# Cosines multiplied on ScalarE, and layer 1's counts emitted later, in a two-layer kernel on one core

## The chip, the core and the metric

The kernel runs as one program on one core of one Trainium2 chip. The metric is the time of one execution on the device, in microseconds. Engines are named as in the profile: PE is TensorE (PEld its weight loads), DVE is VectorE, ACT is ScalarE, POOL is GpSimd, and SP is SyncE, which issues DMAs. A "q" behind a name (SPq, ACTq, POOLq) is that engine's issuing side.

## The reference, cut to what matters

There are two layers over 4 sequences of 1024 tokens with 256 features, all in fp32. In each, an attention part `s` and a mixture of experts `g` work on the same normalized tokens, and their gated product is added to the stream. In layer 0 the attention part is a gated recurrence over the sequence, and the experts are 16 of inner width 128. In layer 1 the projections are cosines, and the experts are 16 of inner width 64, with a shared expert of width 512 beside them. Both choose 4 experts per token, 2 in each of 2 chosen groups of 4 in layer 1.

```python
def _L1_attn_ref(x, theta, W_c, b_c):
    proj = jnp.cos(theta)[None, None] * jnp.cos(xh)        # xh: x by heads of 16
    proj = proj.reshape(Bb, Ss, E)
    scores = jnp.einsum('bse,bte->bst', proj, proj) / jnp.sqrt(jnp.asarray(D, x.dtype))
    attn = jax.nn.softmax(scores, axis=-1)
    out = jnp.einsum('bst,bte->bse', attn, proj)
    return out @ W_c.T + b_c
...
xn = _layernorm(x, axis=-1)
s = _L1_attn_ref(xn, L1_attn_theta, L1_attn_W_c, L1_attn_b_c)
g = _silu(_L1_ffn_ref(xn, L1_ffn_router_w, ...))
x = x + s * g
```

The change concerns the product `cos(theta) * cos(xh)` and the sorting of tokens by expert in `_L1_ffn_ref`.

## The kernel before, in words

**Tiles.** P is 128, S 1024, TB 512, D 256, so KC = 2 halves of the features. A sequence is a "batch" `b` of 0 to 3, worked in halves `q` of 512 tokens. `xnT` holds the normalized activations transposed, 2 x 128 x 1024, and `projT` the cosines in the same shape.

**Preparation.** `prep1(b)` (L967) makes projT and the values. For each half of the features and of the tokens `cos_reduced` (L173: rows L175, L177, L181 twice, L184) brings the angles into range on DVE. Then ACT takes the sine of both feature halves (L995; sine and sigmoid-like functions need different tables, so ACT_TABLE_LOAD rows stand around it). Then DVE multiplies each feature half, 128x1024, by a column of `cth` (L998). After that 32 matmuls on PE (L1006) make the values in PSUM, `projT` times `W_c`, and ACT copies them out (L1013). `val` goes to tiles shared with other users of the pool.

**Routing of layer 1.** `route1` (L908) normalizes (`norm_transposed`, L190: statistics L199 and L200, Newton steps L204 to L216 on DVE, then y on ACT at L226, transposes on PE at L235, copies L237 and L239), computes the logits, and leaves the choices of a batch in `em1` (L926). `places1(h)` (L933) is called for each of two groups of batches: `places` (L359) counts, with matmuls of `em` on PE (L370, L372) and then some forty small instructions on DVE (L376 to L443), at which row each token goes. `dispatch1(h)` (L936) then has POOL scatter the tokens' rows to `rows_in`, and the experts of layer 1 (L1179) work on them.

**Other work near it.** `experts` (L596) holds both layers' expert loop: it transposes a group of 128 rows (L630, copied by L634), multiplies by gate and up weights (L642), applies the gate (L468, L469, L653), transposes h (L659, copied by L661 on ACT), multiplies by the down weights (L667) and copies out (L679, L685); the store of rows is L718. `gathered` (L722) has POOL gather layer 0's expert rows (L725), and DVE adds them up (L790, L792), with a residual that is loaded by L112 as `g_half`. `attend(b)` (L1018) is the attention proper (L1059 to L1118, with L1033 to L1040 finishing a half), `share(b)` (L1127) the shared expert (products L1138 and L1154). `clears` (L841) writes zeros to `rows_in`. Layer 1's weights are loaded at L1360 to L1364.

**What sets the order.** Every such piece of work is a Python generator. It emits instructions and yields a number, the planned microseconds until its next piece. One main line of work at a time is run by `run` (L887), which moves a clock on by a fixed cost for every step (PAIR 0.81, ATTEND 1.4, SHARE 2.6, ROUTED 0.64), and lets the side lines, objects of class `Beside` (L867), emit what is due by then. SETTLED is 3.0 and PIECE is 1.0; both are only planner time and no instruction. A `Beside` has a `pace` with which its pauses are multiplied. The two side lines that concern the change are `routing`, which holds `places1` and `dispatch1`, with a pace of 0.7 from the end of layer 0's experts on, and `preparing`, which holds `prep1` for one batch. Batch 0 is prepared beside layer 0's experts, batches 1 and 2 beside the attention and the shared expert of the batch ahead of them, and batch 3 beside layer 1's experts:

```python
    for b in range(3):
        preparing = Beside(prep1(b + 1, "gu")) if b < 2 else Beside(loads1())
        run(attend(b), ATTEND, [*others, preparing])
        run(share(b), SHARE, [*others, preparing])
        if b < 2:
            together(preparing)
```

`behind` (L859) lets side work be issued after the newest instruction on each engine. Beyond this, a scheduler of the framework merges the emitted lists of each engine with its own idea of costs, so that a change of the emission moves instructions on several engines. An engine executes its own list in order, and pools of tiles (tags such as "x", "tp", "gu", "mm") set when a tile comes free.

Of the kernel before, what the change touches and what calls it, by code (L numbers as in the profile page):

```python
# [13 lines left out]
ALU = mybir.AluOpType  # L14
# [37 lines left out]
SETTLED = 3.0  # L52
PIECE = 1.0
# [10 lines left out]
def two_layer_kernel(  # L64
# [18 lines left out]
    nc = tc.nc  # L83
# [9 lines left out]
    def bank(tag, bufs):  # L93
        tag = side[0] if tag == "side" else tag
        return psum.tile([P, 512], F32, tag=tag, name=tag, bufs=bufs)
# [77 lines left out]
    def cos_reduced(dst, src, tmp, parts):  # L173

        nc.vector.tensor_scalar(tmp, src, INV_2PI, MAGIC, ALU.mult, ALU.add)  # L175
        yield
        nc.vector.tensor_scalar(tmp, tmp, MAGIC, None, ALU.subtract)  # L177
        yield
        at = src
        for part in parts:  # L180
            nc.vector.scalar_tensor_tensor(dst, tmp, -part, at, ALU.mult, ALU.add)  # L181
            at = dst
            yield
        nc.vector.scalar_tensor_tensor(dst, dst, -1.0, dst, ALU.mult, ALU.max)  # L184
# [57 lines left out]
    def transposed_tile():  # L242
        return work.tile([P, KC, S], F32, tag="xnT", name="xnT", bufs=3)
# [324 lines left out]
    def spent(us):  # L568

        clock[0] += us  # L570
# [358 lines left out]
    def tiles_of(h):  # L929

        return slice(GROUPS[h][0] * NT, (GROUPS[h][-1] + 1) * NT)

    def places1(h):  # L933
        placed1.append((yield from places(em1[:, tiles_of(h), :], G1 + h, WE1, "tp")))

    def dispatch1(h):  # L936
# [30 lines left out]
    def prep1(b, tag):  # L967

        if b < 2:
            while b not in turned:  # L970
                yield PIECE
            xnT = turned[b]
        else:
            while b not in routed_done:
                yield PIECE
            xnT = transposed_tile()
            nc.sync.dma_start(out=xnT.rearrange("p k s -> p (k s)"), in_=normedT[b])
            there = clock[0] + LANDING
            while clock[0] < there:
                yield PIECE  # L980
        if b == 1:

            projT = [work.tile([P, QUAD, D + INFO], F32, tag="q", name="projT", bufs=QB) for _ in range(KC)]
            projT = [t.rearrange("p i d -> p (i d)")[:, 0:S] for t in projT]
        else:
            projT = work.tile([P, KC, S], F32, tag="big_a", name="projT", bufs=1)
            projT = [projT[:, kc, :] for kc in range(KC)]
        for kc in range(KC):
            for cols in (slice(0, TB), slice(TB, S)):
                k = work.tile([P, TB], F32, tag="t", name="k", bufs=1)  # L990
                for _ in cos_reduced(projT[kc][:, cols], xnT[:, kc, cols], k, TWO_PI_NORMED):
                    pass
                yield 2 * PIECE
        for kc in range(KC):
            nc.scalar.activation(projT[kc], projT[kc], AF.Sin, bias=half_pi, scale=-1.0)  # L995
        yield PIECE
        for kc in range(KC):
            nc.vector.tensor_scalar(projT[kc], projT[kc], cth[:, kc : kc + 1], None, ALU.mult)  # L998
        yield 3 * SETTLED

        val = [xpool.tile([P, NS, D + INFO], F32, tag="x", name="val", bufs=XB)[:, :, 0:D] for _ in range(NQ)]
        for c in range(0, NT, 2):
            ps = bank(tag, 2)
            for i in range(2):
                for kc in range(KC):
                    nc.tensor.matmul(  # L1006
                        ps[:, i * D : (i + 1) * D],
                        lhsT=projT[kc][:, (c + i) * P : (c + i + 1) * P],
                        rhs=wc_sb[:, kc, :],
                        start=(kc == 0),  # L1010
                        stop=(kc == KC - 1),
                    )
            nc.scalar.copy(val[c // NS][:, c % NS : c % NS + 2, :], ps.rearrange("p (c d) -> p c d", d=D))  # L1013
            spent(1.7)
            yield PIECE
        ready[b] = xnT, projT, val
# [289 lines left out]
    cth = const.tile([P, KC], F32, tag="cth", name="cth")  # L1306
# [28 lines left out]
    def until(ready, *beside):  # L1335

        while not ready():
# [8 lines left out]
    routing = Beside(  # L1346
        then(
            *(step for h, bs in enumerate(GROUPS) for step in (routes1(bs, "side"), places1(h))),
            *(dispatch1(h) for h in range(len(GROUPS))),
        )  # L1350
    )
    preparing = Beside(prep1(0, "side"))
    with behind():
        run(experts0(), PAIR, [clearing, combined, routing, preparing])
# [21 lines left out]
# [6 lines that stand above are left out]
    until(lambda: len(placed1) == len(GROUPS) and preparing.done, *others, preparing)  # L1382
    preparing = Beside(prep1(3, "gu"))

    gating = Beside(then(*(gated1(b) for b in range(B))), 1.7)
# [72 lines left out]
```

## Time and profile before

| | |
|---|---|
| Times of three runs | 1134.44, 1134.29, 1133.79 us (median 1134.29) |
| The profiled execution's own time | 1132.03 us |
| Its span in the profile | 1130.3 us |
| Busy, DVE and POOL | 652.7 us (58%) and 564.4 us (50%) |
| Busy, weight loads of PE | 765.9 us (68%) |
| DMA | 264.82 MB, 234 GB/s over the span |
| Mean granted clock of PE | 0.957 |

The span is what the profiler's records cover, and the execution's own time has about 1.7 us around it. Busy times leave out waiting, issuing of DMAs and semaphores. A line of a timeline reads: start, length, engine, source line, operation, output and inputs, shape, count, and in brackets the idle time of the engine ahead of it with what ended it. "The chain" is the list of instructions and transfers that ended last, followed back from the end; its shares say which engine the time went through.

### The profile page before, as it was taken

The numbers are of one execution on the slowest core, as the hardware profiler recorded it, in microseconds if no ns is written. First come the engines' busy times: TensorE is split into PE (matmuls) and PEld (weight loads), VectorE is DVE, ScalarE is ACT, GpSimd is POOL, SyncE is SP. The second block draws the span as 40 slices with busy tenths as digits, with TensorE's granted clock in tenths as the row PEclk, the third lists the DMA queues.
The fourth block names the chain that finished last, engine by engine and source line by source line (L and its number), as shares of the span: only waits on it lengthen the run. The fifth ranks groups of instructions, "written<-read, shape, count | busy, mean of one in ns | idle before, by whom it ended". The sixth has DMA issues, their size and how long they took to land.

```text
span 1130.3 us, 16158 instructions
## 1 busy us (share of the span) xinstructions
PE 1029.2 (91%) x4928; PEld 765.9 (68%) x4928; DVE 652.7 (58%) x1967; ACT 463.9 (41%) x1028; POOL 564.4 (50%) x589
## 2 busy tenths in 40 slices
PE   5678699999899799979589999999999999999997
PEld 4245368888778688666357765776777777776675
DVE  4866963333688733067977884023733337776666
ACT  3345454444355444331223621221655555553132
POOL 1277377741770000377334677777756666776000
PEclk9868899999999899998699999999999999999999
DMA  8997569999999487997236553654555569994871
GB/s 338 401 410 265 172 191 324 308 310 250 313 346 263 136 215 189 342 246 196 84 119 217 181 175 130 215 196 158 179 170 186 190 215 351 359 332 145 274 242 38
DMA packets 118995, 264.82 MB, mean 234 GB/s; under 512 B 14208, under 2 KB 71680, under 8 KB 117632
## 3 DMA queue, kind: packets, MB, share of 16 engines
q1 hardware_dynamic: 78256, 138.79, 39.3%
q0 software_dynamic: 27264, 75.86, 19.9%
q10 hardware_dynamic: 13392, 49.14, 12.8%
q8 instruction: 43, 0.70, 0.3%
q14 instruction: 40, 0.33, 0.1%
HBM read 119.34 MB, written 144.39 MB: 233 GB/s over the span
## 4 chain that ended last, share of the span: by engine, by line
PE 64%; DVE 21%; DMA 7%; issue 3%; ACT 2%; POOL 2%; DVEq 0%; ACTq 0%; POOLq 0%
PE gu L642 14%; PE acc L667 10%; PE acc L1091 7%; PE tp L630 5%; PE gu L1138 4%; PE acc L1154 4%; PE mm L1138 4%; PE mm L1059 4%; DMA r<-rows_out,row 3%; PE tp L659 3%; PE acc L296 2%; DVE x_half L1243 2%; DMA rows_out<-o 2%; PE mm L514 1%; DVE stats L199 1%
## 5 line engine op out<-in xcount | busy, mean ns | idle before, releaser
L725 POOL DMA_INDIRECT r<-rows_out,row x128 | 130.6, 1021 | 237.5 <-issue 156.5
L642 PE MATMUL gu<-w_sb,xT 128*128 x1280 | 238.0, 329 | 1.5 <-ACT xT L634 0.9
L642 PEld LDWEIGHTS gu<-w_sb,xT 128*128 128x128 f32 x1280 | 193.9, 192 | 15.9 <-issue 2.2
L1205 POOL DMA_INDIRECT results<-o,dest x160 | 159.7, 998 | 76.9 <-issue 29.4
L582 POOL DMA_INDIRECT rows_in<-x_half,row x128 | 134.2, 1048 | 102.7 <-issue 52.4
L667 PE MATMUL acc<-w_sb,hT 128*128 (+1 forms) x640 | 180.1, 397 | 4.0 <-ACT hT L661 4.0
L469 DVE SCALAR_TENSOR_TENSOR h<-sg,gu 128x256 f32<-128x256 f32 (+1 forms) x160 | 56.0, 351 | 161.4 <-ACT sg L468 161.2
L582 POOL DMA_INDIRECT rows_in<-t_half,row x128 | 126.0, 985 | 40.6 <-issue 38.3
L667 PEld LDWEIGHTS acc<-w_sb,hT 128*128 128x128 f32 (+1 forms) x640 | 107.3, 189 | 31.9 <-issue 15.8
L1091 PE MATMUL acc<-val,es 128*128 128x256 f32 x512 | 127.9, 392 | 0.8 <-ACT es L1071 0.8
L634 ACT COPY xT<-tp 128x512 f32<-128x512 f32 x160 | 93.7, 586 | 73.8 <-PE tp L630 71.3
L1091 PEld LDWEIGHTS acc<-val,es 128*128 128x128 f32 x512 | 97.5, 198 | 24.3 <-issue 10.3
L630 PE MATMUL tp<-ident,xs 128*128 128x128 f32 x640 | 101.0, 281 | 0.0
L468 ACT ACTIVATE sg<-gu 128x256 f32<-128x256 f32 (+1 forms) x160 | 53.0, 331 | 113.7 <-PE gu L642 108.6
L630 PEld LDWEIGHTS tp<-ident,xs 128*128 128x128 f32 x640 | 74.4, 142 | 32.5 <-issue 18.1
L685 DVE COPY o<-acc 128x512 f32<-128x512 f32 x80 | 55.0, 688 | 61.4 <-PE acc L667 60.2
L659 PE MATMUL tp<-ident,h 128*128 128x128 f32 (+1 forms) x320 | 62.1, 276 | 10.1 <-DVE h L653 7.8
L1059 PE MATMUL mm<-projT 128*128 128x512 f32 (+3 forms) x192 | 70.0, 487 | 0.0
L661 ACT COPY hT<-tp 128x256 f32<-128x256 f32 (+1 forms) x160 | 58.5, 366 | 25.6 <-PE tp L659 23.8
L1138 PE MATMUL gu<-xnT,w_sb 128*128 128x512 f32 x128 | 61.7, 603 | 5.2 <-ACT val L1013 3.7
L1138 PE MATMUL mm<-xnT,w_sb 128*128 128x512 f32 x128 | 61.8, 608 | 0.3 <-DVE act L469 0.3
L1154 PE MATMUL acc<-w_sb,act 128*128 128x256 f32 x256 | 60.0, 380 | 1.2 <-DVE act L1148 1.2
(225 smaller groups left out, 1449.3 us busy)
## 6 DMA issues: line engine op xcount, KB each, us to landing
rows_in<-zeros SPq DMA_DIRECT2D x20, 1044.0 KB, 14.5
xs<-rows_in SPq DMA_DIRECT2D x40, 512.0 KB, 6.0
rows_out<-o ACTq DMA_DIRECT2D x40, 512.0 KB, 7.4
xs<-rows_in ACTq DMA_DIRECT2D x37, 522.0 KB, 4.0
r<-results SPq DMA_DIRECT2D x32, 512.0 KB, 5.3
rows_in<-zeros SPq DMA_DIRECT2D x1, 12288.0 KB
rows_in<-zeros SPq DMA_DIRECT2D x1, 8192.0 KB
w_sb<-in_w_dram SPq DMA_DIRECT2D x4, 1536.0 KB, 16.8
```

The costliest lines, as they stand in the source:

```text
L582: nc.gpsimd.indirect_dma_start(out=view, out_offset=bass.IndirectOffsetOnAxis(ap=row[:, c0 + s, k : k + 1], axis=0), in_=tokens[:, s, :], ...
L630: nc.tensor.transpose(tp[:, at : at + P], xs[:, j % per * 2 + i, kc * P : (kc + 1) * P], ident)
L634: nc.scalar.copy(xT.rearrange("p i k t -> p (i k t)"), tp)
L642: nc.tensor.matmul(ps[:, i * 2 * hid : (i + 1) * 2 * hid], lhsT=xT[:, i, kc, :], rhs=w_sb[:, bass.ds(off + kc * 2 * hid, 2 * hid)], start= ...
L659: nc.tensor.transpose(tp[0:hid, i * P : (i + 1) * P], h[:, i, :], ident)
L667: nc.tensor.matmul(ps[:, i * D : (i + 1) * D], lhsT=hT[0:hid, i * P : (i + 1) * P], rhs=w_sb[0:hid, bass.ds(expert(2 * j + i) + 4 * hid, D ...
L725: nc.gpsimd.indirect_dma_start(out=r[:, k, :], out_offset=None, in_=rows_out[g], in_offset=bass.IndirectOffsetOnAxis(ap=row[:, c, k : k + ...
L1059: nc.tensor.matmul(ps[:, at:TB], lhsT=projT[kc][:, t * P : (t + 1) * P], rhs=projT[kc][:, q * TB + at : (q + 1) * TB], start=(kc == 0), st ...
L1091: nc.tensor.matmul(av[s // 2][:, (s % 2) * D : (s % 2 + 1) * D], lhsT=es[:, s * P : (s + 1) * P], rhs=val[t // NS][:, t % NS, :], start=(t ...
L1138: nc.tensor.matmul(ps, lhsT=w[:, kc, j * P : (j + 1) * P], rhs=xr[:, kc, :], start=(kc == 0), stop=(kc == KC - 1),)
L1154: nc.tensor.matmul(ys[s // 2][:, (s % 2) * D : (s % 2 + 1) * D], lhsT=h[:, s * P : (s + 1) * P], rhs=ds1_sb[:, j, :], start=(j == 0 and s ...
L1205: nc.gpsimd.indirect_dma_start(out=views[g - G1][QUAD * q + i], out_offset=bass.IndirectOffsetOnAxis(ap=dest[:, i : i + 1], axis=0), in_=o ...
```

## The change

`places1` first yields two SETTLED, 6.0 us of planner time (4.2 at a pace of 0.7), so that the counts of both groups are emitted later. In `prep1` the pause after the sines is two PIECE instead of one, and the two multiplies that follow are done by ACT with the same column as a scale, instead of DVE. Nothing else in the source changes; the eight multiplies are the only instructions that change engine. The lines of `prep1` behind it move down by two or three.

```diff
@@ -931,6 +931,8 @@
     def places1(h):
+
+        yield 2 * SETTLED
         placed1.append((yield from places(em1[:, tiles_of(h), :], G1 + h, WE1, "tp")))
@@ -993,9 +995,10 @@
         for kc in range(KC):
             nc.scalar.activation(projT[kc], projT[kc], AF.Sin, bias=half_pi, scale=-1.0)
-        yield PIECE
+        yield 2 * PIECE
+
         for kc in range(KC):
-            nc.vector.tensor_scalar(projT[kc], projT[kc], cth[:, kc : kc + 1], None, ALU.mult)
+            nc.scalar.mul(projT[kc], projT[kc], cth[:, kc : kc + 1])
         yield 3 * SETTLED
```

## The prediction

> **What bounds the kernel now.** I read the page's busy times and its chain first, then the PE timeline around each place where projT is used, then ACT's timeline and the windows there. About 0.2% of the time, 2.3 us, is what a measurement of this kernel can tell from no change.
>
> ```profile
> PE 1029.2 (91%) x4928; PEld 765.9 (68%) x4928; DVE 652.7 (58%) x1967; ACT 463.9 (41%) x1028; POOL 564.4 (50%) x589
> ...
> PE 64%; DVE 21%; DMA 7%; issue 3%; ACT 2%; POOL 2%; DVEq 0%; ACTq 0%; POOLq 0%
> ```
>
> The first row is busy time by engine, the second the chain that ended last. PE is busy for 91% of the span and carries 64% of the chain; ACT is busy for 41% and carries 2%. So moving DVE work to ACT matters only where PE waits for one of the two. The PE timeline shows these waits (start, length, instructions, and in brackets the idle time before and its releaser):
>
> ```profile
> 383.15 8.55 PE L1006 MATMUL mm<-wc_sb,projT 128*128 128x256 f32 x28 [4.85 <-DVE projT L998]
> ...
> 543.49 1.22 PE L370 MATMUL tp<-em,before__110 128*128 128x256 f32 x2 [5.51 <-DVE em L926]
> ...
> 559.33 6.61 PE L1006 MATMUL gu<-wc_sb,projT 128*128 128x256 f32 x16 [6.68 <-DVE projT L998]
> ...
> 571.34 3.12 PE L1138 MATMUL gu<-xnT,w_sb 128*128 128x512 f32 x4 [3.68 <-ACT val L1013]
> ...
> 813.16 1.13 PE L667 MATMUL acc<-w_sb,hT 64*128 x4 [1.07 <-ACT hT L661]
> ...
> 820.81 1.13 PE L667 MATMUL acc<-w_sb,hT 64*128 x4 [1.30 <-ACT hT L661]
> ```
>
> Batch 0's values (383.15), layer 1's counts (543.49), batch 1's values (559.33) and the shared pass behind batch 1's values (571.34) each wait several microseconds; batch 3's preparation, beside layer 1's experts, costs only 1.07 and 1.30, both for an hT copy on ACT. The rows of the two neighbours, multiply and sine (min/median/max ns):
>
> ```profile
> L998 DVE TENSOR_SCALAR projT<-projT,cth x8: 701/748/925, 366.9 to 819.0; 128x1024 f32<-128x1024 f32 x8
> ```
>
> ```profile
> L995 ACT ACTIVATE projT<-projT,half_pi x8: 1132/1150/1151, 365.7 to 817.8; 128x1024 f32<-128x1024 f32 x8
> ```
>
> **Part 1, the multiply itself.** Eight DVE instructions of 0.748 us go: 6.0 us of DVE. Eight ACT ones come. (Lines are those of before.) The trace has no ACT multiply of 128x1024. The nearest row is the sine, same shape and engine: 1.15 us. Below: ACT's L1075 took 0.60 on 128x512 and 0.38 on 128x256, so 256 columns cost 0.22, and 128x1024 would take 0.60 + 0.44 = 1.04. Above: two L533 at 0.722 (128x512) are 1.44. I take 1.15: 9.2 us of ACT in all. Neither matters by itself (3.2 us of total work more, on an engine with 59% free); the five places below do.
>
> **Part 2, batch 0's preparation (363 to 392).** The second multiply ended at 383.10 on DVE, behind a sine that ended at 382.2. With the first multiply (1.15) ahead on ACT, the table load ends at 381.4 and the sine at 382.5; in the built order of the changed kernel an xT copy (0.57) stands next, then the multiply, 1.15: 384.2. The values at 383.15 start 1.1 later. The gate and hT copy near 369 come later too, but PE's wait there lies ahead of one of 4.85 us and eats into it. Sum +1.2, bounds 0 (the scheduler's copy fits elsewhere) to +2 (both delays add).
>
> **Part 3, the start of attention (450 to 511).** Emitting the counts later shifts everything the scheduler merges there. Two effects on the chain, which runs from the last expert store (454.39, landing after 11.28 us) through the gathers on POOL to the update of DVE at 495.46:
>
> ```profile
> 454.25 0.60 ACT L226 ACTIVATE y<-g_half,shift,rstd 128x256 f32<-128x256 f32 x1
> 454.39 0.33 ACTq L718 DMA_DIRECT2D rows_out<-o  x1
> ```
>
> ACT executes the store of rows_out behind the y step of L226. In the built order the statistics and Newton rows of that half (about 3.5 us of small DVE rows, done at 388.8 before) come on DVE behind the last o copy (451.19 to 451.88), so y and the store behind it issue at about 455.5: +1.15. Against it, SP's queue: two loads of g_half (1 MB), before at 455.10 behind 5.5 MB of layer 1's weights, now stand right behind the L841 clears at 427, so 1 MB less lies in the full stretch (338 to 346 GB/s in the page's slices): up to 3.1 us. What it can free on the chain are POOL's two waits for gathers (0.97 and 1.17) and the last gather's landing of 7.87 against a median of 6.1: 3.9 at most, and I take half, −1.95. The four sv rows of L1038 (0.47 each) partly leave the chain: −0.6, and DVE's rows between batch 1's scores and its em sum to 23.74 instead of 24.35: −0.6. Together −2.0; bounds −4.0 (3.9 and 1.2 gained, 1.15 lost) to +1.2 (store alone).
>
> **Part 4, batch 1 (511 to 576).** DVE is the bound here: in the first window it is busy for 5.40 of 5.40 us while PE stands.
>
> ```profile
> 538.00:543.40 5.40, 0.00 (x0) 0.00 (x0) 5.40 (x25) 0.63 (x1) 4.16 (x4) 0.81 0.36 99
> 571.30:576.00 4.70, 4.67 (x14) 2.78 (x15) 1.45 (x3) 0.55 (x2) 0.00 (x0) 0.64 0.76 223
> 806.00:822.00 16.00, 13.14 (x80) 9.55 (x79) 12.15 (x37) 12.92 (x21) 11.64 (x13) 1.00 0.41 135
> ```
>
> (Columns: length, busy us of PE, PEld, DVE, ACT, POOL with instructions, granted PE clock, DMA share, GB/s.) Two shared products more (1.72 us) now come ahead of the counts, and the last cosine row (L184) comes 2.5 us of DVE work behind em instead of 8.4, since the counts' DVE work (L376 to L443) has moved behind it. Table load 1.28, two sines 2.19 and two multiplies 2.3 follow on ACT; the values could start at em + 8.8, against em + 16.0 before: 7.2 us earlier. But the next wait is then another one:
>
> ```profile
> 568.74 2.07 ACT L226 ACTIVATE y<-g_half,shift,rstd 128x256 f32<-128x256 f32 x4 [10.66 <-DVE shift L216]
> ```
>
> The values' copies L1013 and the transposes L235 stand behind y, and y waits for DVE's shift (L216, 568.54). DVE has all its counts, updates and norms to do before that row, in any order: the built order puts it at em + 26.1 (25.35 before). In the new PE order the transposes L235 stand ahead of the shared pass, so PE stops there until shift, two y, two val and two y: em + 28.5 to 29.2, against em + 28.0 for the L1138 at 571.34. What is gained at 559.33 is given back at 571: +0.6, bounds −2 to +3.
>
> **Part 5, batch 2 (618 to 690).** The counts of the second half now come behind 11 shared products instead of 4, with the 16 value products behind them. PE hides it but for two waits on mm banks (1.3 to 1.8 in my replay), less the 1.16 us stall at 681.80 that shrinks: +0.5, bounds −1 to +3.5.
>
> **Part 6, batch 3 (806 to 835), beside layer 1's experts.** Here ACT is the tight engine: 12.92 of 16 us busy in the third window.
>
> ```profile
> 808.83 1.28 ACT L995 ACT_TABLE_LOAD   x1
> 810.12 1.15 ACT L995 ACTIVATE projT<-projT,half_pi 128x1024 f32<-128x1024 f32 x1
> 811.29 1.28 ACT L468 ACT_TABLE_LOAD   x1
> 812.58 0.28 ACT L468 ACTIVATE sg<-gu 128x128 f32<-128x128 f32 x1
> 812.76 0.35 ACT L661 COPY hT<-tp 64x256 f32<-64x256 f32 x1
> ```
>
> PE waits at 813.16 for the hT copy at 812.76, which is behind a table load, a sine and a second load. The built order puts the multiply on the same queue ahead of the hT copy, in both halves; DVE's L998 lay beside. Each copy comes 1.15 later, and what comes between shifts with it: replaying the order with before's durations, the first wait is 1.07 + 1.15 + 0.2 = 2.4, the second 1.30 + 1.15 + 0.45 = 2.9, and the gate's 0.36 becomes 0.6, so 5.9 against 2.73: +3.2. The values' last product, at the end of the same stretch, loses 0.3 more: +3.5. Bounds: 2.0 (two multiplies, less the 0.3 that two gaps of ACT absorb) to 4.9 (the waits stretched by one 128x512 copy each, 2 x 0.59, and 0.2).
>
> Clock: after its wait of 3.68 us PE was granted 0.64 for 4.7 us (second window row), a loss of 0.36 x 4.7 = 1.7; with waits up to 1.30 it had 1.00 (third). Where between them the point lies, the trace doesn't say; I take 2.4 and 2.9 as below it, and the last rival prices the other case. In sentences apart: the Trainium skill ("TensorE: Matmul & The Clock Gate", section "Part 1: The HAM clock gate") has the clock halved after one idle window of about 3.4 us, until PE has been busy for about as long again. By the rule 2.4 and 2.9 cost nothing and the sum stays at +3.8; the row of 3.68 agrees with it.
>
> **Sum.** +1.2 −2.0 +0.6 +0.5 +3.5 = +3.8; the rest (571 to 1121, gating and expert quads a little reordered on a busy PE) 0 ± 1.5. The profiled execution took 1132.03 us (span 1130.3), so 1135.8 there. The median of the runs shown is 1134.29, 2.3 above it: 1138.1.
>
> **Rivals.** Faster (0.30): batch 1's gain stays. PE's waits of 6.68 and 0.33 at 559 and 550 go (7.0), and the 16 value products, which took 6.61, run at the rate of batch 0's 28 in 8.55, 4.9; of these 1.7 I count 1.0: −8.0 in place of +0.6, so −4.8 in all, 1129.5. For it: the stall is large and ACT idle (0.63 of 5.40). Against: the shift row. It decides if shift ends by about em + 19 instead of em + 26.
>
> No change (0.18): batch 3's multiplies are covered. ACT had gaps of 1.37 (815.13), 0.76 and 1.21 (822 to 824), and PE could fill with values. Then part 6 is 0: +0.3, 1134.6. Against: 12.92 of 16.
>
> Slower by more (0.14): batch 3's waits pass the point at which the clock falls. The 4.85 us wait in batch 0 was followed by a lower clock too (28 products in 8.55 us, against 5.35 for 24 at 823.92). Two losses of 1.7, one for each half, give +7.2: 1141.5. It decides on a wait between 1.30 and 3.68.
>
> That the counts aren't 6 us later, as the diff reads, is certain in part: the built order moves them by 2 and by 7 shared products (1.7 and 6.0 us), which parts 4 and 5 use.
>
> **Numbers.** The forecast has 0.38, since four of its five places rest on a replay of the built order with before's durations; with the rivals: faster 0.30, same 0.18, slower 0.52 (0.38 + 0.14). The parts' bounds, added as squares, give −4.4/+5.5 around 1138.1; to hold 8 in 10 over both signs the range reaches to 1129.0, just below the faster rival, and to 1143.5, the upper bound; about half of the faster rival's chance and a third of the dearer one's lie outside. The slower forecast's own range is 1134.6 to 1143.
>
> **What would show it.** Right: in the changed profile, PE's wait for projT at about 559 is gone and a wait of similar size for y or val stands at 565 to 572; the waits for hT at 813 and 821 are above 2 us each; the ACT multiply takes about 1.15. Wrong: no such wait behind batch 1's values (faster); waits for hT unchanged (same); a granted clock below 0.9 in 806 to 835 (slower).

## The result and the profile after

The changed kernel took 1149.12 us (median of 4 runs, 1147.77 to 1154.81) against 1134.37 for the kernel before: a ratio of 1.0136, with a 95% interval of 1.0110 to 1.0162. Its profiled execution took 1147.77 us with a span of 1146.1, so 15.8 us more span than before. The forecast had the direction, and 3.8 us; the time lies above its range.

The page after: busy time of PE, and the chain that ended last.

```profile
PE 1037.0 (90%) x4928; PEld 768.3 (67%) x4928; DVE 644.7 (56%) x1959; ACT 472.3 (41%) x1036; POOL 562.4 (49%) x589
...
PE 63%; DVE 21%; DMA 8%; ACT 3%; issue 3%; POOL 2%; DVEq 0%; ACTq 0%; SPq 0%; POOLq 0%
```

PE's busy time is up by 8 us (1029.2 before) although it executes the same 4928 matmuls, so about half of the loss is work that ran slower and the other half is waiting. The multiply on ACT cost what the forecast took (1.15):

```profile
L1001 ACT ACTIVATE projT<-projT,cth x8: 1132/1137/1147, 369.7 to 829.8; 128x1024 f32<-128x1024 f32 x8
```

PE's timeline at the places that the prediction showed of before:

```profile
372.64 0.66 PE L659 MATMUL tp<-ident,h 128*128 128x128 f32 x2 [3.84 <-DVE h L653]
...
388.57 3.68 PE L1009 MATMUL mm<-wc_sb,projT 128*128 128x256 f32 x8 [4.65 <-ACT projT L1001]
...
558.87 3.90 PE L1009 MATMUL gu<-wc_sb,projT 128*128 128x256 f32 x16 [1.15 <-ACT projT L1001]
...
576.41 1.18 PE L235 MATMUL tp<-ident,y 128*128 128x128 f32 x4 [10.64 <-ACT y L226]
...
824.64 0.38 PE L659 MATMUL tp<-ident,h 128*64 128x128 f32 x2 [2.53 <-ACT xT L634]
...
831.20 0.41 PE L659 MATMUL tp<-ident,h 128*64 128x128 f32 x2 [2.03 <-ACT hT L661]
```

In batch 0 PE waits 3.84 us near 372 and 4.65 for the multiply. The first was 1.61 before:

```profile
369.41 1.13 PE L667 MATMUL acc<-w_sb,hT 128*128 x4 [1.61 <-ACT hT L661]
```

The wait of 6.68 us ahead of batch 1's values is down to 1.15, and one of 10.64 for y stands 18 us behind it. In batch 3 the two waits are 2.53 and 2.03 (1.07 and 1.30 before). The granted clock of PE ahead of and behind three of these waits is in the windows (columns: stretch, length, busy us of PE, PEld, DVE, ACT, POOL with instructions, PE clock, DMA share, GB/s):

```profile
368.24:371.65 3.41, 0.56 (x3) 0.15 (x1) 1.77 (x6) 3.40 (x7) 0.00 (x0) 1.00 0.09 36
371.65:378.48 6.83, 5.84 (x17) 4.83 (x18) 6.83 (x22) 2.04 (x5) 0.00 (x0) 0.50 0.21 46
...
822.21:825.62 3.41, 0.98 (x5) 0.75 (x6) 2.71 (x11) 2.67 (x6) 1.39 (x2) 1.00 0.33 83
825.62:829.04 3.42, 3.42 (x15) 2.60 (x13) 1.43 (x4) 2.95 (x3) 1.26 (x2) 0.50 0.94 327
829.04:832.45 3.41, 1.38 (x7) 0.81 (x6) 1.14 (x6) 3.40 (x8) 0.55 (x1) 1.00 0.29 78
832.45:835.86 3.41, 3.41 (x16) 2.77 (x15) 1.04 (x3) 0.94 (x3) 2.50 (x4) 0.50 0.52 201
835.86:839.28 3.42, 3.42 (x18) 2.78 (x18) 1.00 (x5) 1.25 (x4) 1.90 (x3) 1.00 0.23 81
```

Around the wait of 3.84 the clock fell to 0.50 for 6.8 us. In batch 3 it fell twice, to 0.50 for 3.4 us each time: once behind the wait of 2.53 and, after 3.4 us at 1.00, once more behind the wait of 2.03.

The span divided at five events, in microseconds, each taken from the timelines of the profiled executions: the first sine of batch 0, the end of batch 0's last value product, the end of batch 1's em on DVE, the first expert group of layer 1 on PE, the end of batch 3's last value product, the end of the span. The two columns for em are the sum of PE's waits between em and the first transposes of y, and the time of these transposes after em. Each row is one execution. Time up to the first sine differs by up to 6.6 us between kernels whose source is alike there, and the stretch from batch 0's values to em by 3.4 us between two whose source differs only in batch 3 (149.2 in e1, 145.8 in e16).

| kernel | to sine | batch 0 | attention to em | em to layer 1's experts | batch 3 | rest | waits after em | y after em |
|---|---|---|---|---|---|---|---|---|
| before | 365.7 | 26.0 | 151.7 | 248.3 | 37.5 | 301.0 | 10.7 | 30.8 |
| after | 366.7 | 29.8 | 154.9 | 250.3 | 43.8 | 300.6 | 14.0 | 25.0 |
| later counts alone (e1) | 368.9 | 25.4 | 149.2 | 239.4 | 39.3 | 301.4 | 4.0 | 27.6 |
| counts, pause, DVE (e9) | 368.5 | 25.4 | 152.7 | 250.5 | 41.8 | 300.3 | 12.7 | 26.4 |
| counts, ACT (e10) | 366.0 | 28.6 | 150.5 | 242.5 | 43.8 | 301.6 | 4.5 | 26.3 |
| counts, ACT in batches 1 and 2 (e11) | 364.6 | 26.5 | 150.2 | 242.9 | 37.5 | 301.1 | 4.4 | 26.5 |
| pause alone (e13) | 371.2 | 25.3 | 155.3 | 250.8 | 41.8 | 300.3 | 20.8 | 25.8 |
| ACT alone (e14) | 366.4 | 28.7 | 151.2 | 247.4 | 42.4 | 301.4 | 9.8 | 30.2 |

From before to after the stretches differ by +1.0, +3.8, +3.2, +2.0, +6.3 and −0.4.

### The profile page after: what moved, and what is told of

Read it like the earlier page. It is cut to its first block, busy times and chain, and to the rows that moved or that the text cites. A ratio compares the mean times of both kernels' runs of the same rounds, so it can differ in the third digit from the quotient of the medians.

```text
span 1146.1 us, 16154 instructions
## 1 busy us (share of the span) xinstructions
PE 1037.0 (90%) x4928; PEld 768.3 (67%) x4928; DVE 644.7 (56%) x1959; ACT 472.3 (41%) x1036; POOL 562.4 (49%) x589
## 4 chain that ended last, share of the span: by engine, by line
PE 63%; DVE 21%; DMA 8%; ACT 3%; issue 3%; POOL 2%; DVEq 0%; ACTq 0%; SPq 0%; POOLq 0%
PE gu L642 15%; PE acc L667 11%; PE acc L1094 6%; PE tp L630 5%; DMA r<-rows_out,row 4%; PE gu L1141 4%; PE acc L1157 3%; PE mm L1141 3%; PE mm L1062 3%; PE tp L659 3%; PE acc L296 2%; DVE x_half L1246 2%; DMA normed<-y 2%; DVE stats L199 1%; POOL r L725 1%
## 5 line engine op out<-in xcount | busy, mean ns | idle before, releaser
L642 PE MATMUL gu<-w_sb,xT 128*128 x1280 | 242.0, 332 | 1.4 <-ACT xT L634 0.9
L642 PEld LDWEIGHTS gu<-w_sb,xT 128*128 128x128 f32 x1280 | 197.4, 195 | 16.6 <-issue 1.9
L1157 PEld LDWEIGHTS acc<-w_sb,act 128*128 128x128 f32 x256 | 49.3, 194 | 20.4 <-issue 10.7
L659 PEld LDWEIGHTS tp<-ident,h 128*128 128x128 f32 (+1 forms) x320 | 37.4, 127 | 38.2 <-issue 20.7
```

The source lines that it names most:

```text
L642: nc.tensor.matmul(ps[:, i * 2 * hid : (i + 1) * 2 * hid], lhsT=xT[:, i, kc, :], rhs=w_sb[:, bass.ds(off + kc * 2 * hid, 2 * hid)], start= ...
L659: nc.tensor.transpose(tp[0:hid, i * P : (i + 1) * P], h[:, i, :], ident)
L1157: nc.tensor.matmul(ys[s // 2][:, (s % 2) * D : (s % 2 + 1) * D], lhsT=h[:, s * P : (s + 1) * P], rhs=ds1_sb[:, j, :], start=(j == 0 and s ...
```

## The experiments

The change has three edits, and the forecast priced only the first two: the later counts, the multiply on ACT, and, in front of the multiply, a pause of two PIECE instead of one. Theory A held that the ACT multiply costs; theory B that the order shifted by the later counts does; theory C came up after the first four runs: that the one extra microsecond of planner time decides. Ratios are of the runs of each kernel to those of the kernel before on the same chip.

**e1, the later counts alone.**

```diff
     def places1(h):
+        yield 2 * SETTLED
```

> The kernel before with only the later counts (2 SETTLED ahead of places1); the multiply stays on DVE with its pause of one PIECE. Theory A (the ACT multiply is what costs: it stands ahead of hT copies in batches 0 and 3, PE's waits there grow and the granted clock falls after them): within 3 us of before, 1133 to 1137, PE's waits at 369 and 813/821 as before (1.6, 1.1, 1.3). Theory B (the order shifted by the late counts is what costs, by way of the last rows_out store and the gathers behind it): 1142 to 1149, with the gathers on POOL starting later than 470.

Measured: 1126.84 us, ratio 0.9919 (0.9883 to 0.9956). Neither theory had this: the later counts are a gain of 0.8%. PE's timeline behind em (which ended at 543.5), and ACT's:

```profile
553.88 5.41 PE L1008 MATMUL gu<-wc_sb,projT 128*128 128x256 f32 x16 [3.97 <-DVE projT L1000]
559.13 1.88 PE L1140 MATMUL gu<-xnT,w_sb 128*128 128x512 f32 x4
560.84 1.89 PE L1008 MATMUL gu<-wc_sb,projT 128*128 128x256 f32 x8
562.57 1.88 PE L1140 MATMUL mm<-xnT,w_sb 128*128 128x512 f32 x4
564.59 1.99 PE L1008 MATMUL gu<-wc_sb,projT 128*128 128x256 f32 x8
566.42 1.89 PE L1156 MATMUL acc<-w_sb,act 128*128 128x256 f32 x8
568.15 3.17 PE L1061 MATMUL mm<-projT 128*128 128x512 f32 x8
571.16 1.33 PE L235 MATMUL tp<-ident,y 128*128 128x128 f32 x8
```

```profile
557.60 0.59 ACT L1015 COPY val<-gu 128x512 f32<-128x512 f32 x1 [3.08 <-PE gu L1008]
...
569.92 2.07 ACT L226 ACTIVATE y<-g_half,shift,rstd 128x256 f32<-128x256 f32 x4 [0.97 <-DVE shift L216]
```

DVE needs as long from em to the shift row as before (26.4 us after em, 25.3 before, 24.3 in the changed kernel), so y comes within 2.1 us of the same time in all three. But here PE has all 32 of batch 1's value products, 16 products of the shared expert and eight score products ahead of y's transposes (571.16), and ACT copies the first values ahead of y. PE waits 4.0 us in this stretch instead of 10.7.

In the changed kernel the values' copies stand behind the first y's on ACT, and the transposes ahead of the shared expert's next products on PE:

```profile
575.75 1.09 ACT L226 ACTIVATE y<-g_half,shift,rstd 128x256 f32<-128x256 f32 x2 [4.38 <-DVE shift L216]
576.75 1.05 ACT L1016 COPY val<-gu 128x512 f32<-128x512 f32 x2
```

**e2, the changed kernel without the later counts** (pause and ACT multiply).

> The changed kernel without the later counts: multiply on ACT, pause of two PIECE, counts where they were before. Theory A: most of the loss is here, 1143 to 1149, with a PE wait above 3 us near 372 and waits above 2 us in batch 3. Theory B: 1134 to 1140, with the store of the last rows landing as early as before.

Measured: 1152.14, ratio 1.0170 (1.0131 to 1.0209). It loses as theory A has it, and a little more than the upper end; but two edits are in it.

**e3 and e4, one batch's multiply back on DVE**, in the changed kernel: batch 0's (e3), batch 3's (e4).

```diff
-            nc.scalar.mul(projT[kc], projT[kc], cth[:, kc : kc + 1])
+            if b in (0,):        # e4: (3,)
+                nc.vector.tensor_scalar(projT[kc], projT[kc], cth[:, kc : kc + 1], None, ALU.mult)
+            else:
+                nc.scalar.mul(projT[kc], projT[kc], cth[:, kc : kc + 1])
```

> The changed kernel with batch 0's multiply back on DVE (pause of two PIECE and later counts kept). Theory A: batch 0's loss of 3.9 us goes: 1143 to 1146, with the PE wait near 370 at 1.6 as before and full clock behind it. If the loss of batch 0 also set when the last rows_out store falls in line, a further 2 to 4 us go (1140 to 1143). Theory B: 1146 to 1149.

> The changed kernel with batch 3's multiply back on DVE. Theory A: batch 3's loss goes (the waits of 2.53 and 2.03 shrink to about 1.1 and 1.3, and the clock in that stretch stays at 1.00 instead of 0.72): 1143 to 1145. Theory B: 1146 to 1149.

Measured: e3 1145.20, ratio 1.0096 (1.0064 to 1.0129), e4 1149.75, ratio 1.0117 (1.0080 to 1.0153). Batch 0 pays for ACT: in e3 its stretch takes 25.3 instead of 29.8, and the wait near 370 is 1.60 again. In e4 batch 3's stretch goes from 43.8 to 41.9 only, against 37.5 in the kernel before: with the multiply back on DVE 4.4 us of loss stay. That doesn't clear ACT, which by itself costs 4.9 us there (e14 below); the two losses don't add. Each of these kernels leaves a loss near 1%.

**What was left.** The built lists of these kernels showed it: with the multiply on either engine, and the later counts in, the order behind em is nearly that of e1 where the pause is one PIECE, and that of the changed kernel where it is two.

**e5 to e8, first runs of four such kernels.** They fell on a chip on which the kernel before took 1467 us too, with stalls that the profile can't name, so their numbers carry little.

> The changed kernel with all eight multiplies back on DVE, so only the later counts and the pause of two PIECE are left: one planner microsecond more than the kernel with the later counts alone (1126.8). Theory C (the extra PIECE decides the order: in the built lists it puts the norm's rows behind layer 0's last o copy and the values' copies and products behind y): 1138 to 1144, with a PE wait near 10 us for y behind batch 1's first values and the gathers starting 8 us later than with the counts alone. Theory A (the ACT multiply decides): 1125 to 1130.

> The changed kernel with the pause back to one PIECE: later counts and all eight multiplies on ACT. Theory C: batch 1 keeps the gain of the later counts (no wait for y above 3 us there, gathers early), and only batches 0 and 3 pay for ACT, 3.9 and about 5 us on top of 1126.8: 1132 to 1138. Theory A: 1145 to 1150.

> The kernel before with only the pause of two PIECE; multiply on DVE, counts where they were. Theory C: 1140 to 1146, near the run with ACT and the pause but without the later counts (1152.1) less what ACT costs in batches 0 and 3. Theory A: 1132 to 1137, no change.

> Later counts, pause of one PIECE, multiply on ACT in batches 1 and 2 alone and on DVE in batches 0 and 3. If ACT is only dear where its queue is full, this is the best so far: 1122 to 1127, no slower than the later counts alone (1126.8). If the ACT multiply is dear in itself: 1130 or above.

Measured, as ratios: e5 1.0009 (0.9959 to 1.0059), e6 1.0027 (0.9990 to 1.0064), e7 1.0101 (1.0047 to 1.0155), e8 0.9949 (0.9908 to 0.9989). The four were run again, as e9, e10, e13 and e11.

**e9, later counts and the pause, multiply on DVE.**

```diff
     def places1(h):
+        yield 2 * SETTLED
...
-        yield PIECE
+        yield 2 * PIECE
```

> Later counts, multiply on DVE, pause of two PIECE: only the pause stands between this and the kernel with the later counts alone (ratio 0.992). The first run of it fell on a chip where the kernel before took 1467 us, which tells nothing of it. Theory C (the extra PIECE decides the order): 1138 to 1144, a PE wait near 10 us for y behind batch 1's first values. Theory A (the ACT multiply decides): 1125 to 1130.

Measured: 1144.62, ratio 1.0079 (1.0050 to 1.0107). The pause, added to the later counts, turns their gain of 0.8% into a loss of as much. PE's timeline in batch 1:

```profile
561.12 6.75 PE L1009 MATMUL gu<-wc_sb,projT 128*128 128x256 f32 x16 [8.17 <-DVE projT L1001]
...
572.98 0.93 PE L235 MATMUL tp<-ident,y 128*128 128x128 f32 x4 [3.39 <-ACT y L226]
```

The waits are 8.17 for the multiply, which stands behind counts and statistics on DVE, and 3.39 for y. On ACT the multiply shortened the first (1.15 in the changed kernel) and lengthened the second (10.64): y came when DVE was through, in both.

**e10, later counts and ACT in all batches, pause of one.**

> Later counts, multiply on ACT in all batches, pause of one PIECE, for the same reason again. Theory C: batch 1 keeps the gain of the later counts, and batches 0 and 3 pay 3.9 and about 5 us for ACT: 1132 to 1138. Theory A: 1145 to 1150.

Measured: 1135.27, ratio 1.0009 (0.9978 to 1.0041). This is what ACT costs at the better order: 0.9% against e1. Batches 0 and 3 take 3.2 and 4.5 us longer than in e1, since PE waits there for hT copies and what hangs on them:

```profile
810.62 0.38 PE L659 MATMUL tp<-ident,h 128*64 128x128 f32 x2 [2.58 <-ACT xT L634]
...
817.18 0.64 PE L659 MATMUL tp<-ident,h 128*64 128x128 f32 x2 [3.64 <-ACT hT L661]
```

**e11, later counts, ACT in batches 1 and 2, pause of one.** The edit is that of e3 with `if b in (0, 3)`, and the pause of one.

> Later counts, pause of one PIECE, ACT in batches 1 and 2, DVE in 0 and 3. If ACT is dear only where its queue is full: 1122 to 1127. If the ACT multiply is dear in itself: 1130 or above.

Measured: 1125.18, ratio 0.9922 (0.9893 to 0.9951). As fast as e1: on ACT or on DVE, in these two batches the multiply makes no difference that shows.

**e12, later counts by three SETTLED.**

> The kernel with the later counts alone, delayed by 3 SETTLED instead of 2; multiply on DVE, pause of one PIECE. In its built order all of batch 1's values are copied ahead of y, and the shared pass's first four down products too. Theory C (what counts is what stands behind y): 1122 to 1127, as good as 2 SETTLED or a little better. If the gain hung on that one order: 1130 or above.

Measured: 1171.99, ratio 1.0305 (1.0255 to 1.0355). Wrong by 45 us. POOL's timeline:

```profile
618.89 0.94 POOL L725 DMA_INDIRECT r<-rows_out,row  x1 [41.24 <-DVE y L792]
```

POOL's gathers of layer 0's rows waited 41.24 us for DVE's additions, which this order has further back, and the rows' updates, the norms and the second half's y waited with them (PE waits of 13.83 and 19.72 for y, at 663 and 685). Which row of the order does it stays open.

**e13, the pause alone.**

> The kernel before with only the pause of two PIECE. Theory C (the extra PIECE costs, by what it puts ahead of what): in the built order the transposes of y stand ahead of all of batch 1's values, as in the run with ACT and the pause but without the later counts (ratio 1.017), and batch 3 pays 4.3 as with the later counts: 1141 to 1150, ratio 1.006 to 1.014. Theory C' (the pause only takes away what the later counts gained): 1134 to 1139, ratio at most 1.004.

Measured: 1145.05, ratio 1.0081 (1.0055 to 1.0107). The pause costs without the later counts too. PE's timeline in batch 1:

```profile
570.86 3.78 PE L1059 MATMUL mm<-projT 128*128 128x512 f32 x4 [17.89 <-DVE projT L998]
577.55 2.16 PE L235 MATMUL tp<-ident,y 128*128 128x128 f32 x8 [2.91 <-ACT y L226]
```

All transposes of y stand ahead of all values there, and PE waits 20.8 us in the two waits shown.

**e14, ACT alone**, pause of one, counts as before.

> The multiply on ACT in all batches, nothing else: counts and pause as before. From the runs with the later counts (1135.3 with ACT everywhere, 1125.2 with ACT in batches 1 and 2) ACT in batches 0 and 3 costs 2 to 4 and 6 to 8 us, and batches 1 and 2 nothing: 1142 to 1148, ratio 1.007 to 1.011. If ACT in batch 1 gains by itself (PE's 6.68 us wait for the multiply on DVE goes): 1136 to 1141.

Measured: 1138.95, ratio 1.0031 (1.0007 to 1.0054). The time lies in the second range, but not for its reason: batches 0 and 3 pay 2.7 and 4.9 us by the table, and the stretch from em gets 0.9 back, not the 6.7 of the wait for the multiply.

**e15, the 4 MB of weights later**, on top of e1.

```diff
-    nc.sync.dma_start(out=we1_sb, in_=w1)
...
         run(attend(b), ATTEND, [*others, preparing])
+        if b == 0:
+            nc.sync.dma_start(out=we1_sb, in_=w1)
```

> The later counts alone (ratio 0.992), and the load of layer 1's 4 MB of expert weights is issued behind batch 0's attention instead of ahead of it, next to the last rows_out store. If the DMA traffic at 455 to 480 holds up the gathers and the update behind them: the store lands 5 us earlier or more, PE's waits near 498 and 508 (2.5 and 2.9) shrink, 1120 to 1126. If the gathers are bound by POOL's own issue (1.25 us each): no change, 1125 to 1130.

Measured: 1131.71, ratio 0.9975 (0.9950 to 1.0000), slower than e1 (the intervals just touch). The last store of rows_out landed after 7.8 us instead of 11.2, and the gathers started 71.6 us after batch 0's values instead of 75.0, but PE then waited longer:

```profile
503.38 0.47 PE L1069 MATMUL mm<-ident,es 128*128 128x128 f32 x1 [8.02 <-ACT es L1077]
```

Against 2.49 in e1. The load, issued at 468.68, fell on the gathers themselves: between 489 and 498 DVE waited 2.88, 3.95 and 3.41 us for gathered rows (2.17 at most in e1). An earlier start of the gathers bought nothing there.

**e16, e18 and e17: the pause in one batch only**, on top of e1: batch 3, 0 and 1.

```diff
-        yield PIECE
+        yield 2 * PIECE if b == 3 else PIECE      # e18: b == 0, e17: b == 1
```

> The later counts alone (ratio 0.992), with the pause of two PIECE in batch 3 only; multiply on DVE. Theory C for batch 3: its stretch from the first expert group of layer 1 to the last value takes 4.3 us more, with a PE wait of 2.5 for the row numbers (dest) near 810: 1129 to 1133, ratio 0.995 to 0.998. If batch 3's 4.3 us came from what the pause did further ahead: 1125 to 1129.

> The later counts alone (ratio 0.992), with the pause of two PIECE in batch 0 only; multiply on DVE. In the built order the norm's rows come behind layer 0's last o copy, so that the gathers start 8 us later, but all sixteen value products of batch 1 still come ahead of y's transposes. Theory C, placed in batch 1: most of the gain stays, 1125 to 1131, ratio 0.992 to 0.997. If the late store and gathers matter: 1134 to 1142.

> The later counts alone (ratio 0.992), with the pause of two PIECE in batch 1 only; multiply on DVE. In the built order four of batch 1's values' transposes of y come ahead of the second eight value products, as in the changed kernel. Theory C, placed in batch 1: the gain of the later counts goes, 1134 to 1142, ratio 1.000 to 1.007, with PE waits of 8 us or more in all between em and the second half's first blocks. If the pause of batch 0 is the one that matters: 1125 to 1129.

Measured: e16 1125.75, ratio 0.9923 (0.9892 to 0.9954); e18 1137.35, ratio 1.0012 (0.9989 to 1.0035); e17 1129.29, ratio 0.9942 (0.9915 to 0.9968). In e16 batch 3's stretch took 44.5 us against 39.3 in e1, with waits as expected and one more,

```profile
800.19 0.38 PE L659 MATMUL tp<-ident,h 128*64 128x128 f32 x2 [2.58 <-DVE dest L1201]
...
810.54 0.38 PE L659 MATMUL tp<-ident,h 128*64 128x128 f32 x2 [2.45 <-DVE h L653]
```

but the time shows nothing of it: the execution that was profiled made it up ahead of em (145.8 against 149.2). Whether batch 3's pause costs is open. Batch 1's pause costs 0.2%, which the intervals don't tell from nothing, batch 0's 0.9%, the other way round than expected. In the traces both show at one place. PE in batch 1, e18 and then e17:

```profile
569.63 1.18 PE L235 MATMUL tp<-ident,y 128*128 128x128 f32 x4 [9.42 <-ACT y L226]
```

```profile
559.99 2.50 PE L1008 MATMUL gu<-wc_sb,projT 128*128 128x256 f32 x5 [10.01 <-DVE projT L1000]
```

So the pause of batch 0, some 170 us earlier in the program, moves y's transposes ahead of the shared expert's next products in batch 1 (waits after em: 12.1 us), as the pause of batch 1 leaves the values late (11.6). The time of e18 lies in the range that was given for late gathers, but by this trace they are the smaller part: e18's stretch up to em is 2.3 us longer than e1's, that from em to layer 1's experts 7.9. (The profiled execution of e18, 1132.05 us, is 5 us under its median, so the trace may miss a part of what it costs.)

## Why the prediction was wrong

The span grew by 15.8 us, not by 3.8. Of the 12 us that are missing, the table has 5.2 at the start of attention, 2.8 in batch 3, 2.6 in batch 0, 0.9 in batches 1 and 2, and 1.0 ahead of everything that was changed; the rest, 0 ± 1.5, came out at −0.4. The steps that failed are the credit of 1.95 at the start of attention, the full clock behind waits of 2.4 and 2.9 in batch 3, and the second multiply's time in batch 0. Behind much of it stands an edit that the forecast gave no term.

**The edit that wasn't priced.** The forecast replayed the built order of all three edits and took its shape for the doing of the counts and the multiply. Alone, the later counts gain 0.8%, the pause costs 0.8%, ACT costs 0.3%; counts and pause together cost 0.8%, so between these two the effects don't add. Had the one PIECE been taken out, the change would have made no difference (e10), and with ACT in batches 1 and 2 only, besides, it would have gained 0.8% (e11).

**Batch 1 (+0.6) and batch 2 (+0.5): near.** From em to layer 1's experts the change took 2.0 us. PE's wait for projT shrank to 1.15 and one for y took its place, by the mechanism that was forecast, with the shared expert's products behind the transposes at em + 26.0 (forecast 28.5 to 29.2). What was wrong is the condition for the faster rival: it needed the shift by em + 19. In e1 the shift came at em + 26.4 and the gain stayed, since PE had 23.6 us of work ahead of y's transposes (27.6 less 4.0 of waits), and 11.0 in the changed kernel (25.0 less 14.0). The row to look at was PE's order up to that wait, and not only when the wait ends.

**Batch 0 (+1.2, measured +3.8): the size was off.** The multiply's own delay is there, in ACT's timeline:

```profile
369.72 1.13 ACT L1001 ACTIVATE projT<-projT,cth 128x1024 f32<-128x1024 f32 x1
370.76 0.36 ACT L468 ACTIVATE sg<-gu 128x256 f32<-128x256 f32 x1
371.02 0.36 ACT L661 COPY hT<-tp 128x256 f32<-128x256 f32 x1
```

It stands ahead of a gate and an hT copy, and the forecast had PE's wait near 369 eaten by the next one. But the wait grew to 3.84, PE ran at 0.50 behind it (5.8 us of work, so at most 2.9 us lost), and the second wait, 4.65, was nearly as long as before (4.85). DVE's last cosine came 15.3 us after the first sine in both kernels. What came later is ACT's second table load, since it stands behind a copy of o that waits for PE's products. Before and after:

```profile
378.34 0.59 ACT L679 COPY o<-acc 128x512 f32<-128x512 f32 x1 [0.48 <-PE acc L667]
378.94 1.28 ACT L995 ACT_TABLE_LOAD   x1
```

```profile
383.95 0.59 ACT L679 COPY o<-acc 128x512 f32<-128x512 f32 x1 [0.48 <-PE acc L667]
384.56 1.28 ACT L997 ACT_TABLE_LOAD   x1
```

So the first wait delayed the second multiply instead of being eaten by the wait for it. The rival with the falling clock was put in batch 3 and had its first case here. With a pause of one the stretch takes 28.6 and 28.7 (e10, e14), 29.8 with two.

**Start of attention (−2.0, measured +3.2 up to em): the sign was wrong.** The store came 1.0 us later against the value products, as forecast (1.15). But it had been issued 0.24 us ahead of the 4 MB weight load (454.39 and 454.63) and now comes behind it. SP's queue before, and after, and then ACT's:

```profile
454.63 0.43 SPq L1364 DMA_DIRECT2D w_sb<-in_w_dram  x1
```

```profile
459.50 0.42 SPq L1367 DMA_DIRECT2D w_sb<-in_w_dram  x1
```

```profile
460.24 0.60 ACT L226 ACTIVATE y<-g_half,shift,rstd 128x256 f32<-128x256 f32 x1 [1.01 <-DVE shift L216]
460.30 0.33 ACTq L718 DMA_DIRECT2D rows_out<-o  x1
```

The store took 16.7 us to land instead of 11.28, and POOL's first gather, at 466.75 before, came 6.4 us later against the value products (81.4 us behind the last of them, 75.1 before):

```profile
477.98 0.94 POOL L725 DMA_INDIRECT r<-rows_out,row  x1 [134.37 <-DMA normed<-y]
```

The line names another DMA, but in every kernel listed below whose store has a recorded landing the first gather starts 0.9 to 1.1 us behind it. The two loads of g_half did move ahead, as forecast (431.45), and 1 MB less in the stretch didn't bring the store in earlier. So the credit of 1.95 was the failed step.

It is the pause that does this, and not the later counts, to which the forecast put it. Leaving out e5 to e8, which ran on the slow chip, in all seven kernels with a pause of two in batch 0 (after, e2, e3, e4, e9, e13, e18) the store is issued 0.8 us behind the load and lands after 16.4 to 19.3 us, the gathers start 81.1 to 84.0 us after batch 0's values, and the stretch up to em takes 151.5 to 158.8. In the eight with a pause of one and the load in its place (before, e1, e10, e11, e12, e14, e16, e17) the store is 0.24 us ahead and lands after 11.2 or 11.3 where the landing is on record, the gathers start after 73.8 to 75.6, and the stretch takes 145.8 to 151.7. How much of the +3.2 the late store itself makes stays open: in e15 the gathers were the earliest of all, and the stretch took 154.4.

**Batch 3 (+3.5, measured +6.3): the mechanism of the waits was right, the clock wasn't.** The waits grew by 1.8 us to 4.56, not to 5.9, but the clock fell behind each of the two. By the windows the loss is at most 2 x 0.5 x 3.41 = 3.4, which is what the dearest rival had set for it (two losses of 1.7); 1.1 of the 6.3 isn't traced. It isn't the multiply's alone: the stretch takes 41.8 with the multiply on DVE and the pause of two (e9, e13), 42.4 and 43.8 with ACT and a pause of one (e14, e10), and 43.8 with both.

**The clock.** The forecast held 2.4 and 2.9 for safe. The Trainium skill ("TensorE: Matmul & The Clock Gate", section "Part 1: The HAM clock gate") has the clock halved after one idle window of about 3.4 us. Here it was halved although PE had been busy for 0.98 and 1.38 of the 3.41 us ahead (the windows above), so the measurement decides, and shorter waits are enough in this case. Nor is there one length of wait up to which it is safe. Before, waits of 1.07 and 0.36 near 813 left the clock at 1.00. In e1 the same two waits, in the same order of work, were followed by 0.50 for 6.8 us:

```profile
804.37 1.13 PE L667 MATMUL acc<-w_sb,hT 64*128 x4 [1.07 <-ACT hT L661]
...
805.87 0.38 PE L659 MATMUL tp<-ident,h 128*64 128x128 f32 x2 [0.37 <-DVE h L653]
```

```profile
803.19:806.60 3.41, 1.98 (x12) 1.28 (x10) 3.41 (x12) 2.02 (x6) 2.71 (x3) 1.00 0.45 120
806.60:813.43 6.83, 6.71 (x26) 5.38 (x26) 3.13 (x9) 5.31 (x8) 5.39 (x5) 0.50 0.48 173
```

In these windows the clock changes in steps of 3.41 us and their double, so it may matter where a wait falls against the steps; no run tests that.

## What to carry to other kernels

Price every edit of a change on its own, a scheduler's pause too: build the order with each one taken out, and only then replay. Where one engine's result ends a wait at a fixed time, what counts is how much work stands ahead of the waiting instruction, so compare the work queued up to it, not the wait's end. A transfer that moves by a microsecond can move past another one that is four megabytes long.

## What the runs showed of the hardware

PE's granted clock was 1.00 or 0.50 in the windows shown, and changed in steps of 3.41 us or twice that. It fell behind single waits of 2.53 and 2.03 us in the changed kernel, and in e1 behind waits of 1.07 and 0.37 us that had left it at 1.00 in the kernel before. An ACT multiply of 128x1024 by a column takes 1.137 us, the DVE one 0.74 (e9), so the move trades 0.74 us for half as much again. A 512 KB store issued 0.8 us behind a 4 MB load of another queue landed after 16.4 to 19.3 us (seven kernels), one issued 0.24 us ahead of it after 11.2 or 11.3, and 7.8 with the load moved away (e15).
